# The eighth key group of the attention by seven products too, with another order of products and all four banks taken out by ScalarE

## The chip, the cores and the metric

The kernel runs on one core of a Trainium2 chip. Its engines work side by side, each through its own instruction queue in order: TensorE (PE in the profile; its weight loads are listed apart as PEld), VectorE (DVE), ScalarE (ACT), GpSimd (POOL) and SyncE (SP), which here only issues DMAs. SBUF is the working memory; PSUM holds what TensorE writes. The metric is the device time in microseconds of one execution; before the change it is 3199.19 us, the median of three runs (3198.45 to 3201.14).

## The reference

Two layers on an input x of 4 x 256 x 64 x 64, all fp32. Layer 0 is a self-attention over the N = 4096 positions of an image; layer 1 is a clustering block with an MLP and two pointwise convolutions, which the change hardly touches.

```python
xf = x.reshape(B, Cc, N)
q = jnp.einsum('oc,bcn->bno', wq, xf) + bq
k = jnp.einsum('oc,bcn->bon', wk, xf) + bk[None, :, None]
attn = jax.nn.softmax(jnp.einsum('bnd,bdm->bnm', q, k), axis=-1)
v = jnp.einsum('oc,bcn->bon', wv, xf) + bv[None, :, None]
out = jnp.einsum('bcn,bmn->bcm', v, attn).reshape(B, Cc, H, W)
return gamma[0] * out + x
```

## The kernel before

**Tiling.** An image (batch) is worked as 8 query blocks of 512 queries (`NB`); each block goes through 8 key groups of 512 keys (`RG` = 4 tiles of 128 keys). One block with one group is a unit: 64 units per image, numbered u, with block nb = u // 8 and group g = u % 8. The four images follow one another. While one image is in its clustering block and MLP, the values and first scores of the next are worked in between.

**A unit's life.** `half` (L452) computes half of a unit's scores, two matmuls (`products`, L420); ScalarE copies them to an SBUF slot (`kept`, L433), and VectorE folds them into a running maximum (`highest_of`, L444). The score PSUM pool has two buffers, and one of them is held for the whole attention by the tile `hold`, so there is one buffer left for scores: the next score matmuls wait for copy and maximum. Scores run up to 11 units ahead; `at` says at which point of which unit each half is due (two per unit, three in four early ones). When a block's maxima are complete, `fold`, `highest` and `rows` bring the maximum across the partitions by way of a DMA through DRAM, and `known` (L566, ScalarE) copies it to `hold[:, 0]`; for block 1, `spread` does it with TensorE instead.

**Weights of the softmax.** `exps(u)` subtracts the maximum (L583, VectorE, two instructions) and takes the exponentials (ScalarE). `factors(u)` makes what the products need: t31 (L616, VectorE, which also reads `hold[:, 1]`), the B12 sum, t4 and the row sums `one` and `both` (POOL, L595). t31 has two buffers, t4 one.

**Seven products.** For groups 0 to 6 the product of values and weights, split into 2 x 2 quarters, is done with seven quarter products instead of eight (a Strassen-Winograd scheme). `weigh(u, av, part)` issues them in four parts, (1, 5), (7, 2), (6, 4), (3), each product as two 128x256 matmuls, which the profile counts as four records (L679). They are summed in four PSUM banks over the groups of the block. Their key-side sums (`sums`, POOL) are made once per image. Group 7 is multiplied plainly: 128x512 matmuls (L657), into banks 2 and 3 only.

**Taking the banks out.** Banks 0 and 1 are complete after group 6. At the start of unit 7 `evict` (L699, ScalarE) scales both into an SBUF tile, `combine` (L709 to L712, four operations) adds the quarters up, on POOL in blocks 0 to 5 and on VectorE in blocks 6 and 7, and `gather` (POOL) ends the row sums. Banks 2 and 3 are added by `complete` (L724, VectorE), half at the end of unit 7, half in the next block's unit 0. `total`, `leave` and `sent` then divide by the row sums and send the block out to DRAM in units 1 to 5 of the next block. In block 7 the end differs: no scores are due, inputs are loaded back with an accumulating DMA that POOL issues (L772, L777), VectorE takes statistics, and the row sums are turned by two small TensorE products (L1003, L1017).

**Order.** The whole order is written by hand in `weighting` (L881): for each unit, which instruction is issued before which. In unit u stand, in turn: scores due at part 0, evictions and `gather` (unit 7), `exps(u + 1)`, maxima, part 0 of the products, scores due at part 1, part 1, scores due at part 2, `known` (unit 6), `factors(u + 1)`, maxima, part 2, `leave` and `sent`, part 3, `tail`. Waits between engines are set by the framework from what each instruction reads and writes.

Of the kernel before, what the change touches and what calls it, by code (L numbers as in the profile page):

```python
# [8 lines left out]
F32 = mybir.dt.float32  # L9
# [24 lines left out]

SEVEN = 7
QW = NB // 2
B21, B11, B12, B22 = range(4)
PAIR = slice(B11, B12 + 1), slice(B21, B22 + 1, 3)


PC = [
# [12 lines left out]
def attention_then_cluster_block(  # L54
# [250 lines left out]
    def attention(b, xs, ys):  # L305


        own = {}
        stats = small.tile([P, 2 * NBLK, 6], F32, tag="stats", name=f"st1_{b}")
        cells = small.tile([P, KC, NBLK, 4], F32, tag="cells", name=f"cells_{b}")  # L310
        qs, ks, slots, mxs, accs, tops, rdens, ts = {}, {}, {}, {}, {}, {}, {}, {}
# [265 lines left out]
        def exps(u, between=lambda: None):  # L577

            s = slots[u]
            mb = own["hold"][:, 0].rearrange("p (h n) -> p h n", h=2).unsqueeze(2)  # L580
            for j in range(2):
                sh = s[:, PAIR[j]]
                nc.vector.tensor_tensor(sh, sh, mb.to_broadcast([P, 2, 2, QW]), ALU.subtract)  # L583
                if j == 0:
                    between()
            if u % GRP < SEVEN:
                b12 = own["hold"][:, 1].rearrange("p (r n) -> p r n", r=2)
                nc.scalar.activation(b12, s[:, B12], AF.Exp)  # L588
                nc.scalar.activation(s[:, B11], s[:, B11], AF.Exp)  # L589
            else:  # L590
                nc.scalar.activation(s[:, PAIR[0]], s[:, PAIR[0]], AF.Exp)
            nc.scalar.activation(s[:, PAIR[1]], s[:, PAIR[1]], AF.Exp)  # L592
# [4 lines left out]
        def factors(u):  # L597

            nb, g = divmod(u, GRP)
            s = slots[u]
            if g == 0:
                accs[nb] = work.tile([P, 2, 2, QW], F32, tag="acc", bufs=1, name=f"acc_{b}_{nb}")
            one, both = accs[nb][:, 0], accs[nb][:, 1]
            if g >= SEVEN:
                if g == SEVEN:
                    plus(both, both, one, ALU.subtract)
                for acc, q in ((both, B11), (one, B12), (both, B21), (one, B22)):
                    eng = nc.vector if acc is one and nb == NBLK - 1 else nc.gpsimd  # L610
                    eng.tensor_tensor(acc, acc, s[:, q], ALU.add)  # L611
                return
            b12 = own["hold"][:, 1].rearrange("p (r n) -> p r n", r=2).unsqueeze(1)
            t31[u] = work.tile([P, 2, 2, QW], F32, tag="t13", name=f"t13_{b}_{u}")
            t4s[u] = work.tile([P, 2, QW], F32, tag="t4", bufs=1, name=f"t4_{b}_{u}")
            nc.vector.tensor_tensor(  # L616
                t31[u], s[:, B11 : B22 + 1 : 2], b12.to_broadcast([P, 2, 2, QW]), ALU.add
            )
# [29 lines left out]
        def weigh(u, av, part):  # L648

            g, s = u % GRP, slots[u]  # L650
            if g >= SEVEN:
                c = part // 2
                for t in (0, 1) if part % 2 == 0 else (2, 3):

                    apart = c == 1 and g == SEVEN and t == 0
                    for h in (slice(0, 1), slice(1, 2)) if apart else (slice(0, 2),):
                        nc.tensor.matmul(  # L657
                            av[2 + c].rearrange("p (h n) -> p h n", h=2)[:, h],
                            own["v"][:, RG * g + t, c * P : (c + 1) * P],
                            s[:, PAIR[t // 2], t % 2][:, h],  # L660
                            start=False,
                            stop=(g == GRP - 1 and t == RG - 1),
                        )
                return
            a11, a12, a21, a22 = left(g)
# [9 lines left out]
            }  # L675
            for i in ((1, 5), (7, 2), (6, 4), (3,))[part]:
                bank, half_, a, t = terms[i]
                for r in range(2):
                    nc.tensor.matmul(  # L679
                        av[bank][:, half_ * QW : (half_ + 1) * QW],  # L680
                        a[:, r],
                        t[:, r],
                        start=(g == 0 and r == 0 and i in (1, 7, 2, 4)),
                        stop=(g == SEVEN - 1 and r == 1 and i in (5, 6)),
                    )
# [8 lines left out]
        def evict(nb, av, i):  # L694


            if i == 0:
                ts[nb] = work.tile([P, 4, QW], F32, tag="t", bufs=1, name=f"t_{b}_{nb}")
            nc.scalar.activation(  # L699
                ts[nb][:, (slice(0, 4, 3), slice(1, 3))[i]],  # L700
                av[i].rearrange("p (h n) -> p h n", h=2),
                AF.Identity,
                scale=pvc("gamma"),
            )

        def combine(nb, eng):

            t = ts[nb]
            eng.tensor_tensor(t[:, 1], t[:, 1], t[:, 0], ALU.subtract)  # L709
            eng.tensor_tensor(t[:, 3], t[:, 1], t[:, 3], ALU.subtract)  # L710
            eng.tensor_tensor(t[:, 1], t[:, 1], t[:, 2], ALU.add)
            eng.tensor_tensor(t[:, 2], t[:, 2], t[:, 3], ALU.add)  # L712

        def complete(nb, av, c):

            t = ts[nb]
            for dst, src, op in (
                ((t[:, ::3], av[2].rearrange("p (h n) -> p h n", h=2), ALU.add),),
                (
                    (t[:, 1], av[3][:, :QW], ALU.subtract),  # L720
                    (t[:, 2], av[3][:, QW:], ALU.add),
                ),
            )[c]:
                nc.vector.scalar_tensor_tensor(dst, src, pvc("gamma"), dst, ALU.mult, op)  # L724

# [83 lines left out]
        def alone():  # L809
# [25 lines left out]
            fold(0)  # L835
            for g in range(4, SEVEN):
                for f in sums(g):
                    f()
# [8 lines left out]
            exps(0)  # L847
            factors(0)

        def maximum():  # L850
# [30 lines left out]
        def weighting(next_x, fill, early, begin):  # L881

            mb, av, den, peak = None, None, iter(()), iter(())

# [22 lines left out]
            for u in range(units):  # L907
# [5 lines left out]
                if g == 0:  # L913
                    done, av = av, [
                        pool.tile([P, NB], F32, tag=tag, name=f"av{c}_{b}_{nb}")
# [19 lines left out]

                if nb and g == 0:
                    complete(nb - 1, done, 1)
                elif nb and g == 1:
                    den = total(nb - 1)
# [54 lines left out]
                if g == GRP - 1 and more:  # L994
                    complete(nb, av, 0)
                tail(u)
# [36 lines left out]
        parts.ys, parts.alone, parts.weighting = ys, alone, weighting  # L1033
        parts.factors, parts.sums = factors, [lambda g=g, i=i: sums(g)[i]() for g in range(SEVEN) for i in range(4)]
        parts.score, parts.fold, parts.q_block, parts.k_unit = score, fold, q_block, k_unit
# [10 lines left out]
    def cluster(b, ys, stats, cells, rest, fill, gelu, nxt, maxima, turn):  # L1046
# [278 lines left out]
        fill(0 if nxt else 1)  # L1325
        stats2 = small.tile([P, 2 * NBLK, 6], F32, tag="stats", name=f"st2_{b}")
        pieces = {}
# [186 lines left out]
    def mlp(b, ys, stats2, fill, nxt, blocks, turned, maxima):  # L1514
# [314 lines left out]
        for nb in range(blocks):  # L1829
            end = nb == blocks - 1  # L1830
            for j in range(4):
# [12 lines left out]
                if nxt and nb:  # L1844
                    for _ in range(2 if j == 0 else 1):
                        if nxt.sums:
# [192 lines left out]
```

## Time and profile before

| what | value |
|---|---|
| median of three runs | 3199.19 us |
| the profiled execution | 3196.98 us |
| its span, first to last instruction | 3195.0 us |
| mean granted TensorE clock | 0.990 |
| POOL operation 128x512 (L595, into acc) | 352 of 1329 ns |
| POOL operation 128x256 (L709, L711, L712) | 24 each of 727 to 730 ns |
| VectorE t31 (L616) | 224 of 1217 ns |
| ScalarE eviction (L699) | 64 of 689 ns |
| plain products of group 7 (L657) | 448 of 592 ns, 128 of 378 ns |
| an average middle query block | 57.8 us |

A profile page lists for each engine its busy time and its share of the span. A timeline line gives the start in us, the duration in us, the engine, the line of the kernel, the operation, what it writes and reads, the shape and how many instructions are merged; in brackets stands how long the engine had been idle and what ended that. The granted clock is the share of full speed that TensorE was given. All fences marked as profile are copied from the profile and not shortened.

### The profile page before, as it was taken

The page shows a single profiled execution, that of the slowest core. Times are in us where ns is not written, and L with a number is a line of the kernel's source. Part 1 is how long each engine was busy: PE and PEld are TensorE (multiplying, and loading weights), DVE is VectorE, ACT ScalarE, POOL GpSimd, SP SyncE. Part 2 cuts the span into 40 slices and gives each one's busy share as a digit, 9 for nine tenths or more (in the row PEclk, how much of TensorE's full clock was granted, in tenths as well). Part 3 has the DMA queues.
Part 4 walks back from the last instruction along what each step waited for, and adds up shares of the span by engine and source line. Part 5 has one row for each costly group of instructions (what it writes and reads, how often), then busy time and mean ns, then how long its engine had stood idle before and what let it go on. Part 6 is the DMA issues. An engine that isn't in the chain of part 4 may idle for free.

```text
span 3195.0 us, 40473 instructions
## 1 busy us (share of the span) xinstructions
PE 3085.5 (97%) x13890; PEld 2445.7 (77%) x13890; DVE 2537.0 (79%) x3649; ACT 1734.8 (54%) x2719; POOL 2260.6 (71%) x2127
## 2 busy tenths in 40 slices
PE   7999999999999999999999999999999999998999
PEld 5777887788677787768867788786876787875786
DVE  3888888677788888867778888877778888887675
ACT  4556654545556665445555666544556566654444
POOL 3888886378488888547848888855766888883663
PEclk8999999999999999999999999999999999999999
DMA  5122126100112123510011222431111112150000
GB/s 164 40 63 63 60 61 182 63 21 30 47 50 63 53 60 94 155 50 28 23 56 44 66 60 63 111 123 50 30 44 43 54 60 64 56 149 2 14 21 27
DMA packets 105868, 200.33 MB, mean 63 GB/s; under 512 B 14416, under 2 KB 30400, under 8 KB 104128
## 3 DMA queue, kind: packets, MB, share of 16 engines
q1 hardware_dynamic: 101856, 181.94, 17.9%
q0 software_dynamic: 2976, 14.70, 2.5%
q8 instruction: 110, 1.80, 0.2%
q10 hardware_dynamic: 832, 1.11, 0.1%
q14 instruction: 94, 0.77, 0.1%
HBM read 149.37 MB, written 48.34 MB: 62 GB/s over the span
## 4 chain that ended last, share of the span: by engine, by line
PE 42%; POOL 24%; DVE 19%; issue 8%; ACT 6%; DMA 1%; POOLq 0%; SPq 0%; ACTq 0%; DVEq 0%
PE mo L1651 10%; POOL acc L595 9%; PE av L679 6%; PE hq L1734 5%; DVE top L444 5%; DVE s L583 4%; POOL t L595 4%; POOL s L595 4%; DVE t L616 3%; PE hp L1734 3%; PE hr L1734 3%; PE fv L1225 3%; PE sc L420 3%; POOL acc L611 2%; PE vp L375 2%
## 5 line engine op out<-in xcount | busy, mean ns | idle before, releaser
L433 ACT COPY s<-sc 128x1024 f32<-128x1024 f32 x512 | 514.8, 1011 | 506.3 <-PE sc L420 500.1
L583 DVE TENSOR_TENSOR s<-s,hold 128x1024 f32<-128x1024 f32 x512 | 598.7, 1209 | 28.9 <-ACT hold L566 15.0
L595 POOL TENSOR_TENSOR s<-t,s 128x512 f32<-128x512 f32 x224 | 303.5, 1355 | 356.1 <-DVE t L616 287.6
L679 PE MATMUL av<-t,v 128*128 128x256 f32 x1792 | 464.8, 382 | 12.8 <-DVE t L616 11.7
L679 PE MATMUL av<-s,v 128*128 128x256 f32 x1792 | 460.8, 379 | 2.2 <-ACT s L589 2.2
L595 POOL TENSOR_TENSOR acc<-acc,t 128x512 f32<-128x512 f32 x352 | 461.2, 1329 | 0.0
L679 PE MATMUL av<-s,sum 128*128 128x256 f32 x1792 | 459.5, 379 | 0.0
L420 PE MATMUL sc<-q,k 128*128 128x512 f32 x1024 | 405.6, 480 | 36.8 <-DMA k<-k 10.5
L444 DVE TENSOR_TENSOR top<-sc,top 128x1024 f32<-128x1024 f32 x326 | 397.8, 1220 | 29.7 <-ACT s L433 24.8
L1689 ACT ACTIVATE hs<-hs,pv_s 128x256 f32<-128x256 f32 x496 | 232.3, 502 | 343.5 <-DVE hs L1725 343.5
L616 DVE TENSOR_TENSOR t<-s,hold 128x1024 f32<-128x1024 f32 x224 | 272.7, 1217 | 159.3 <-ACT s L592 71.0
L679 PEld LDWEIGHTS av<-t,v 128*128 128x128 f32 x1792 | 338.4, 190 | 70.1 <-DVE t L616 21.4
L1651 PE MATMUL mo<-hs,w 128*128 128x256 f32 x1512 | 385.3, 381 | 0.0
L679 PEld LDWEIGHTS av<-s,v 128*128 128x128 f32 x1792 | 340.3, 190 | 57.8 <-ACT s L589 2.6
L679 PEld LDWEIGHTS av<-s,sum 128*128 128x128 f32 x1792 | 339.4, 189 | 54.5 <-issue 1.9
L1651 PEld LDWEIGHTS mo<-hs,w 128*128 128x128 f32 x1512 | 283.0, 190 | 47.2 <-ACT hs L1689 6.4
L595 POOL TENSOR_TENSOR t<-s 128x512 f32<-128x512 f32 x224 | 295.7, 1320 | 17.6
L420 PEld LDWEIGHTS sc<-q,k 128*128 128x128 f32 x1024 | 176.6, 190 | 144.0 <-DVE top L444 70.2
L592 ACT ACTIVATE s<-s 128x1024 f32<-128x1024 f32 x256 | 267.5, 1045 | 1.2
L1725 DVE TENSOR_TENSOR hs<-hq,hs 128x256 f32<-128x256 f32 x496 | 198.8, 421 | 79.2 <-PE hq L1734 69.3
L588 ACT ACTIVATE hold<-s 128x512 f32<-128x512 f32 x224 | 135.1, 603 | 221.5 <-DVE s L583 221.4
L679 PE MATMUL av<-t,sum 128*128 128x256 f32 x896 | 231.7, 381 | 0.0
(299 smaller groups left out, 5349.1 us busy)
## 6 DMA issues: line engine op xcount, KB each, us to landing
k<-k SPq DMA_DIRECT2D x256, 256.0 KB, 2.7
x<-in_x SPq DMA_DIRECT2D x62, 512.0 KB, 6.6
out<-xn SPq DMA_DIRECT2D x62, 256.0 KB, 2.1
att<-t SPq DMA_DIRECT2D x56, 256.0 KB, 3.9
x<-att POOLq DMA_DIRECT2D x12, 1024.0 KB, 8.7
q<-q SPq DMA_DIRECT2D x32, 256.0 KB, 4.1
w<-in_w SPq DMA_DIRECT2D x8, 1024.0 KB, 10.3
rden<-row_rd SPq DMA_DIRECT2D x28, 256.0 KB, 3.7
```

The lines of the kernel that those rows point to most:

```text
L420: nc.tensor.matmul(sc[:, r, :], k_s[:, (2 * h + r) * P : (2 * h + r + 1) * P], qs[u // GRP], start=True, stop=True,)
L433: nc.scalar.copy(slots[u][:, PAIR[h]].rearrange("p h r n -> p r h n"), tiles(sc))
L444: nc.vector.tensor_tensor(top, src, top if saved[nb] is None else saved[nb], ALU.max)
L583: nc.vector.tensor_tensor(sh, sh, mb.to_broadcast([P, 2, 2, QW]), ALU.subtract)
L592: nc.scalar.activation(s[:, PAIR[1]], s[:, PAIR[1]], AF.Exp)
L595: nc.gpsimd.tensor_tensor(out, x, y, op)
L616: nc.vector.tensor_tensor(t31[u], s[:, B11 : B22 + 1 : 2], b12.to_broadcast([P, 2, 2, QW]), ALU.add)
L679: nc.tensor.matmul(av[bank][:, half_ * QW : (half_ + 1) * QW], a[:, r], t[:, r], start=(g == 0 and r == 0 and i in (1, 7, 2, 4)), stop=(g ...
L1651: return nc.tensor.matmul(bank[:, half * HB : (half + 1) * HB], a[:, j], t, start=start, stop=stop)
L1689: nc.scalar.activation(src, src, AF.Gelu_apprx_tanh, bias=pvc("b1", P, j + 4 * (i > 1)))
L1725: nc.vector.tensor_tensor(dst, ps, term, ALU.add)
L1734: nc.tensor.matmul(out, w, x, start=True, stop=True)
```

## The change

Group 7 is now treated like the others; the special case and its constant go.

- `exps`: group 7 too takes B12's exponential into `hold[:, 1]`: two instructions of 512 in place of one of 1024.
- `factors`: for group 7 t31 on VectorE and four sums on POOL in place of four row-sum additions on POOL (two of them on VectorE in block 7). The last subtraction `both - one` moves from before these to behind them.
- `weigh`: seven products in group 7; the parts become (1, 5), (2, 3), (7, 6), (4), and in an image's last unit (7, 6), (1, 5), (2, 3), (4). Banks 0, 2, 1, 3 are then complete after parts 0, 1, 2, 3 of unit 7.
- In blocks 0 to 6 four evictions on ScalarE, one behind each part of unit 7; the fourth takes half a bank. The quarters are combined by six POOL operations, two at the end of each of units 0, 1 and 2 of the next block. VectorE's completions and its combine of block 6 go.
- In block 7 banks 1 and 0 are evicted behind parts 0 and 1, VectorE combines, and completes with two operations in place of three.
- Four more key-side sums per image: at the start for image 0, in the MLP for the others, where now two sums instead of one are issued at j = 1.
- `stats` and `cells` get one buffer instead of two; a tile `t5` is new, and `w2` serves a further use.

```diff
+ORDER = (1, 5), (2, 3), (7, 6), (4,)
+LAST = (7, 6), (1, 5), (2, 3), (4,)
...
-            if u % GRP < SEVEN:
-                b12 = own["hold"][:, 1].rearrange("p (r n) -> p r n", r=2)
-                nc.scalar.activation(b12, s[:, B12], AF.Exp)
-                nc.scalar.activation(s[:, B11], s[:, B11], AF.Exp)
-            else:
-                nc.scalar.activation(s[:, PAIR[0]], s[:, PAIR[0]], AF.Exp)
+            b12 = own["hold"][:, 1].rearrange("p (r n) -> p r n", r=2)
+            nc.scalar.activation(b12, s[:, B12], AF.Exp)
+            nc.scalar.activation(s[:, B11], s[:, B11], AF.Exp)
             nc.scalar.activation(s[:, PAIR[1]], s[:, PAIR[1]], AF.Exp)
...
-            if g >= SEVEN:
-                if g == SEVEN:
-                    plus(both, both, one, ALU.subtract)
-                for acc, q in ((both, B11), (one, B12), (both, B21), (one, B22)):
-                    eng = nc.vector if acc is one and nb == NBLK - 1 else nc.gpsimd
-                    eng.tensor_tensor(acc, acc, s[:, q], ALU.add)
-                return
...
+            if g == GRP - 1:
+                plus(both, both, one, ALU.subtract)
...
-            for i in ((1, 5), (7, 2), (6, 4), (3,))[part]:
+            for i in (ORDER if u < units - 1 else LAST)[part]:
...
+        def combined(nb):
+
+            t = ts[nb]
+            yield from combine(nb, nc.gpsimd)
+            yield nc.gpsimd.tensor_tensor(t[:, ::3], t[:, ::3], ts.pop((nb, 2)), ALU.add)
+            yield nc.gpsimd.tensor_tensor(t[:, 1], ts.pop((nb, 3))[:, 0], t[:, 1], ALU.subtract)
...
-                if g == SEVEN:
-                    evict(nb, av, 0)
-                    evict(nb, av, 1)
-                    if nb < NBLK - 2:
-                        combine(nb, nc.gpsimd)
+                if g == GRP - 1:
                     gather(nb)
                 if g + 1 < GRP or more:
                     exps(u + 1)
-                if g == SEVEN and nb >= NBLK - 2:
-                    combine(nb, nc.vector)
...
                 weigh(u, av, 0)
+                if g == GRP - 1:
+                    evict(nb, av, 0 if more else 1)
...
                 weigh(u, av, 1)
...
-                if g == GRP - 1 and not more:
-                    complete(nb, av, 0)
+                if g == GRP - 1:
+                    evict(nb, av, 2 if more else 0)
+                    if not more:
+                        for _ in combine(nb, nc.vector):
+                            pass
...
                 weigh(u, av, 2)
+                if g == GRP - 1:
+                    if more:
+                        evict(nb, av, 1)
+                    else:
+                        complete(nb, av, 0)
...
                 if g == GRP - 1 and more:
-                    complete(nb, av, 0)
+                    evict(nb, av, 3)
+                    quarters = combined(nb)
+                elif nb and g < 3:
+                    for _ in range(2):
+                        next(quarters)
                 tail(u)
```

More of the change, by code (lines that the diff above doesn't have):

```diff
@@ L31 @@
 LEAD, SLOTS = 11, 10
-SEVEN = 7
 QW = NB // 2
@@ L308, in attention @@
         own = {}
-        stats = small.tile([P, 2 * NBLK, 6], F32, tag="stats", name=f"st1_{b}")
-        cells = small.tile([P, KC, NBLK, 4], F32, tag="cells", name=f"cells_{b}")
+        stats = small.tile([P, 2 * NBLK, 6], F32, tag="stats", bufs=1, name=f"st1_{b}")
+        cells = small.tile([P, KC, NBLK, 4], F32, tag="cells", bufs=1, name=f"cells_{b}")
         qs, ks, slots, mxs, accs, tops, rdens, ts = {}, {}, {}, {}, {}, {}, {}, {}
@@ L650, in weigh @@
             g, s = u % GRP, slots[u]
[L651 to L664, printed above, removed]
             a11, a12, a21, a22 = left(g)
@@ L683, in weigh @@
                         start=(g == 0 and r == 0 and i in (1, 7, 2, 4)),
-                        stop=(g == SEVEN - 1 and r == 1 and i in (5, 6)),
+                        stop=(g == GRP - 1 and r == 1 and i in (5, 3, 6, 4)),
                     )
@@ L694, in evict @@
         def evict(nb, av, i):
-            if i == 0:
+            if nb not in ts:
                 ts[nb] = work.tile([P, 4, QW], F32, tag="t", bufs=1, name=f"t_{b}_{nb}")
+            if i == 2:
+                ts[nb, 2] = work.tile([P, 2, QW], F32, tag="w2", bufs=1, name=f"t2_{b}_{nb}")
+            if i == 3:
+                ts[nb, 3] = work.tile([P, 1, QW], F32, tag="t5", bufs=1, name=f"t5_{b}_{nb}")
             nc.scalar.activation(
-                ts[nb][:, (slice(0, 4, 3), slice(1, 3))[i]],
-                av[i].rearrange("p (h n) -> p h n", h=2),
+                ts[nb, i] if i > 1 else ts[nb][:, (slice(0, 4, 3), slice(1, 3))[i]],
+                av[i][:, : QW if i == 3 else NB].rearrange("p (h n) -> p h n", n=QW),
                 AF.Identity,
@@ L708, in combine @@
             t = ts[nb]
[L709 to L712, printed above, removed]
+            yield eng.tensor_tensor(t[:, 1], t[:, 1], t[:, 0], ALU.subtract)
+            yield eng.tensor_tensor(t[:, 3], t[:, 1], t[:, 3], ALU.subtract)
+            yield eng.tensor_tensor(t[:, 1], t[:, 1], t[:, 2], ALU.add)
+            yield eng.tensor_tensor(t[:, 2], t[:, 2], t[:, 3], ALU.add)
+        def combined(nb):
[3 more added lines that the diff above has]
+            yield nc.gpsimd.tensor_tensor(t[:, 1], ts.pop((nb, 3))[:, 0], t[:, 1], ALU.subtract)
         def complete(nb, av, c):
             t = ts[nb]
[L717 to L724, printed above, removed]
+            dst, src, op = (
+                (t[:, ::3], av[2].rearrange("p (h n) -> p h n", h=2), ALU.add),
+                (t[:, 1], av[3][:, :QW], ALU.subtract),
+            )[c]
+            nc.vector.scalar_tensor_tensor(dst, src, pvc("gamma"), dst, ALU.mult, op)
         def total(nb):
@@ L835, in alone @@
             fold(0)
-            for g in range(4, SEVEN):
+            for g in range(4, GRP - 1):
                 for f in sums(g):
@@ L848, in alone @@
             factors(0)
+            for f in sums(GRP - 1):
+                f()
         def maximum():
@@ L881, in weighting @@
         def weighting(next_x, fill, early, begin):
-            mb, av, den, peak = None, None, iter(()), iter(())
+            mb, av, den, peak, quarters = None, None, iter(()), iter(()), iter(())
             views = {units - 7 + i: i for i in range(6)}
@@ L913, in weighting @@
                 if g == 0:
-                    done, av = av, [
+                    av = [
                         pool.tile([P, NB], F32, tag=tag, name=f"av{c}_{b}_{nb}")
@@ L934, in weighting @@
                     caught(1)
-                if nb and g == 0:
-                    complete(nb - 1, done, 1)
-                elif nb and g == 1:
+                if nb and g == 1:
                     den = total(nb - 1)
@@ L1033, in attention @@
         parts.ys, parts.alone, parts.weighting = ys, alone, weighting
-        parts.factors, parts.sums = factors, [lambda g=g, i=i: sums(g)[i]() for g in range(SEVEN) for i in range(4)]
+        parts.factors, parts.sums = factors, [lambda g=g, i=i: sums(g)[i]() for g in range(GRP) for i in range(4)]
         parts.score, parts.fold, parts.q_block, parts.k_unit = score, fold, q_block, k_unit
@@ L1325, in cluster @@
         fill(0 if nxt else 1)
-        stats2 = small.tile([P, 2 * NBLK, 6], F32, tag="stats", name=f"st2_{b}")
+        stats2 = small.tile([P, 2 * NBLK, 6], F32, tag="stats", bufs=1, name=f"st2_{b}")
         pieces = {}
@@ L1844, in mlp @@
                 if nxt and nb:
-                    for _ in range(2 if j == 0 else 1):
+                    for _ in range(2 if j < 2 else 1):
                         if nxt.sums:
```

## The prediction

> **What bounds the kernel.** I read the page's first part, then the timeline of single query blocks engine by engine, then the chain of waits inside one block.
>
> ```profile
> PE 3085.5 (97%) x13890; PEld 2445.7 (77%) x13890; DVE 2537.0 (79%) x3649; ACT 1734.8 (54%) x2719; POOL 2260.6 (71%) x2127
> ```
>
> 97% looks like a TensorE-bound kernel, but the records overlap: a 128x256 matmul "takes" 0.38 us while in the timeline four of them start every 0.86 us (331.73, 332.59, 333.45), 0.215 each. By starts, an attention unit (one key group for one query block) costs TensorE 28 x 0.215 = 6.04 us of products and 0.86 for its four score matmuls: 6.9. Its real period is in the timeline of VectorE and ScalarE, units 3 to 4 of batch 0's fourth block:
>
> ```profile
> 338.03 2.34 DVE L583 TENSOR_TENSOR s<-s,hold 128x1024 f32<-128x1024 f32 x2
> 340.29 1.22 DVE L444 TENSOR_TENSOR top<-sc,top 128x1024 f32<-128x1024 f32 x1
> 340.47 0.60 ACT L588 ACTIVATE hold<-s 128x512 f32<-128x512 f32 x1 [0.46 <-DVE s L583]
> 341.00 0.61 ACT L589 ACTIVATE s<-s 128x512 f32<-128x512 f32 x1
> 341.52 1.04 ACT L592 ACTIVATE s<-s 128x1024 f32<-128x1024 f32 x1
> 342.65 1.22 DVE L616 TENSOR_TENSOR t<-s,hold 128x1024 f32<-128x1024 f32 x1 [1.15 <-POOL acc L595]
> 343.89 1.23 DVE L444 TENSOR_TENSOR top<-sc,top 128x1024 f32<-128x1024 f32 x1
> ```
>
> The next subtraction starts at 345.03. A closed ring: subtract 2.34, exponentials 2.1, t sum 1.22, maximum 1.22, hand-overs 0.1: 7.0 us. (342.65 is put down to POOL, which ended at 341.99; the exponentials ended at 342.56.) So VectorE and ScalarE set 7.0, TensorE follows with 6.9, POOL needs four operations, 5.1. Three limits lie close together.
>
> **The removed work.** The eighth group's 18 matmuls (L657) run from 1265.69 to 1272.56, 6.87 us; seven products take 6.04. Saved: 0.83 us x 32 blocks = 26.6 us, if TensorE decided. The page's mean durations say the opposite: 14 x 592 + 4 x 378 ns = 9.8 us before against 28 x 380 = 10.6, which would be 27 us slower. [...] The starts in this trace agree, so I take minus 26.6 as what TensorE has to give. Whether it gets out depends on the ring, unit by unit.
>
> **Units 6 and 7 of blocks 1 to 5.** The timeline of VectorE and ScalarE before:
>
> ```profile
> 359.39 2.30 DVE L583 TENSOR_TENSOR s<-s,hold 128x1024 f32<-128x1024 f32 x2
> 361.62 1.21 DVE L444 TENSOR_TENSOR top<-sc,s 128x1024 f32<-128x1024 f32 x1
> 362.86 2.07 DVE L444 TENSOR_TENSOR top<-s,top 128x1024 f32<-128x1024 f32 x1
> 364.74 0.60 ACT L566 COPY hold<-mr 128x512 f32<-128x512 f32 x1
> 365.04 1.23 DVE L444 TENSOR_TENSOR top<-sc,top 128x1024 f32<-128x1024 f32 x1
> 366.18 2.34 DVE L583 TENSOR_TENSOR s<-s,hold 128x1024 f32<-128x1024 f32 x2
> 368.36 1.27 ACT L699 ACTIVATE t<-av,pv_s 128x512 f32<-128x512 f32 x2
> 371.71 1.22 DVE L616 TENSOR_TENSOR t<-s,hold 128x1024 f32<-128x1024 f32 x1 [1.98 <-ACT s L592]
> 374.27 0.75 DVE L724 SCALAR_TENSOR_TENSOR t<-av,pv_s,t 128x512 f32<-128x512 f32 x1 [0.21 <-POOL t L712]
> ```
>
> The next subtraction is at 374.94. Unit 6 is the one unit whose VectorE list is full (6.79 us) and it has no t sum, since unit 7 needs none. Unit 7 takes 8.76, because the two evictions (1.27) stand before the exponentials and a completion (0.75) follows.
> - Unit 7 after: no eviction ahead of the exponentials, no completion on VectorE. The ring is the ordinary 7.0. Gain 1.76. The evictions now follow the exponentials and the products they read, so ScalarE does them in the slack: two by 5.8 us after the unit's subtraction; behind them waits the second score copy (until 6.7), and behind it TensorE's next scores, which need the maximum at 7.07 anyway. Cost nothing; half a us later it would cost its excess.
> - Unit 6 after: VectorE gains the t sum, 1.22, with no gap to take it. And there is a new wait. The hold tile has two banks; ScalarE's copy L566 writes the first, the t sum reads the second. Are they kept apart? Row L588 above: it writes bank two and waits 0.46 us for the second subtraction, which only reads bank one. And at 729.83 a ScalarE copy of the first bank of an MLP tile starts only when the product in the other bank ends (729.17 + 0.59). So I take it that a PSUM tile is waited for whole, and the t sum comes behind L566, which comes behind the score copy: 5.95 to 6.05 us after the subtraction. Then 1.22 + 1.22 + hand-overs: 8.43 us instead of 6.79. Loss 1.64. If the banks are kept apart, the t sum starts at 5.54 and the unit takes 8.0.
> - Net per block: 1.76 - 1.64 = 0.1 gain (0.55 with banks apart). TensorE's saved 0.83 becomes idle time in unit 6 (some 1.9 us).
>
> **Block 0.** There the maximum comes over TensorE and VectorE idles 2.83 us in unit 6, so the t sum is hidden. Unit 7: 8.57 before; after 7.9, since a held maximum (1.76) fills the exponentials' shadow. Gain 0.6, less 0.1 in the next unit.
>
> **Block 6 into 7, and block 7.** Timeline of batch 1:
>
> ```profile
> 1266.30 2.35 DVE L583 TENSOR_TENSOR s<-s,hold 128x1024 f32<-128x1024 f32 x2 [3.68 <-ACT hold L566]
> 1275.73 1.13 PE L679 MATMUL av<-t,v 128*128 128x256 f32 x4 [2.14 <-DVE t L616]
> 1275.75 1.28 POOL L595 TENSOR_TENSOR s<-t,s 128x512 f32<-128x512 f32 x1 [1.50 <-DVE t L616]
> 1325.06 1.65 POOL L595 TENSOR_TENSOR rden<-acc 128x256 f32<-128x256 f32 x2
> ```
>
> Before, the combine sat on VectorE between subtraction and t sum (1268.64 to 1274.5) and TensorE lost 2.14 us. It goes to POOL; that stall goes. What is late next: eviction 0 stands on ScalarE behind the exponentials and the shift (2.17), and the t sum of unit 7 behind L566, now about 1267.45 because the new exponential order starts after both subtractions. TensorE then waits about 2.2 us for that t sum, and 2.1 us for eviction 0 (1276.0) before block 7's first product. It starts block 7 about 1 us later than before.
>
> Then POOL. Added in block 7: the combine, 4 x 0.73 + 1.33 + 0.75 = 5.0 us in units 0 to 2, and for the eighth group five operations (6.4) in place of one and two (1.59 + 3.45). POOL's idle time in block 7 before was 1.50 + 1.77 + 0.57 + 1.25 + 1.27 + 0.26 = 6.6; block 7 has no scores, units last 6.36, and POOL also issues three back-transfers (0.9 each) and one of 1.08, and does the 2.36 scaling. Walking its queue from 1268.8 with 1.27 per operation, it is busy without a gap from unit 57 on: its B12 sum for the last unit ends near 1323.0, where TensorE, through with the first product of the last list (7, 6), waits some 2 us. The last product ends near 1328.2 (1326.2 before), the row sums (1325.06 + 1.65 before) near 1330.4, the next value projection at about 1331.3 instead of 1328.36. Loss 2.9 us a batch. With banks apart the same walk starts 2.7 earlier and ends with 1.1 lost. The back-transfers are issued up to 4 us later; who needs them first, the pooling of unit 57, reads at about 1284, and the t sum behind it has 3 us of slack.
>
> **The rest.** Four more key-side sums per batch (0.8 us each): in the MLP they go to POOL, which waits 73 us there for TensorE; nothing, at worst 1 us a batch. At the start they fall into a 3.25 us POOL gap. Product order: 4 is now last, so POOL's next t4 waits for the unit's end (about 7.15 us after the subtraction) and would start at 7.28: nothing, by 0.1 us. Single buffers for the statistics: their lives follow one another; nothing.
>
> **The sum.** Per batch: -0.5 - 5 x 0.1 + 2.9 = +1.9; four batches +7.6 us. The profiled execution took 3196.98 (span 3195.0), which becomes 3204.6; that execution lies 2.2 under the median of 3199.19, so 3206.8, say **3207**.
>
> **Rivals.**
> - *TensorE decides* (10%): the ring's slack swallows the t sum, 0.83 gained in every block: 3199.2 - 26.6 = 3172.6. For it: page 97%. Against: unit 6, where TensorE waits for VectorE (the scores at 366.62 came 0.6 late).
> - *Banks kept apart* (15%), on the faster side: the t sum of unit 6 doesn't wait for L566. Per batch -0.5 - 5 x 0.55 + 1.1 = -2.15; 3190.6. It decides from the point at which the t sum starts before 5.95 us of its unit. Against: L588's wait.
> - *POOL's overrun is absorbed* (15%): block 7 loses 1 us instead of 2.9 because back-transfers issue beside other work: about 3199.
> - *The clock drops* (12%): batch 0's gap of 2.20 us was followed by groups of four at 1.97 and 1.91 instead of 1.03, clock 0.83 in that stretch; 2.14 in batch 1 was not. [...] by batch 0's row some 1.75 us each. In half of 24 gaps: +21, 3228. [...] three of the four 2.1 us gaps left no trace.
> - Forecast: 48%, own range 3200 to 3216.
>
> No change means within 0.2%, 6.4 us, which is what a measurement here can tell. Faster 10 + 15 = 25%; same: the absorbed case and a fifth of the forecast, 26%; slower 49%. Range 3186 to 3223: it leaves out the first rival and most of the clock case.
>
> **What would show it.** Unit 6 of blocks 1 to 5 near 8.4 us between subtractions with the t sum right after L566, unit 7 near 7.0; TensorE idle about 1.9 us before unit 7's scores; in block 7 POOL without gaps and the row sums some 3 us later. Wrong: unit 6 below 7.5, or block 7's last product no later than now.

## The result, and the profile after

The changed kernel takes **3241.0 us** (median of four runs, 3239.64 to 3243.07), beside 3199.4 us for the kernel before on the same chip: a ratio of 1.0128, interval 1.0116 to 1.014. It is 42 us slower, where 8 us were forecast; the time lies above the forecast's range. The profiled execution has a span of 3237.8 us, 42.8 more than before.

The first part of its page, busy time of each engine:

```profile
PE 3068.9 (95%) x14210; PEld 2504.8 (77%) x14210; DVE 2502.2 (77%) x3569; ACT 1772.2 (55%) x2807; POOL 2323.0 (72%) x2223
```

PE and VectorE lost busy time, ScalarE gained 37 us, POOL 62; none of the four is busy all the time. So busy times don't explain the 42.8 us, and they are looked for unit by unit. As in the prediction, a unit runs from one subtraction (L586, once L583) to the next. The table sums over the four images how each place differs between the two profiled executions, beside what the prediction's steps make of it. (Its own sum rounds these steps to +7.6.) Each entry is rounded by itself.

| place | forecast, us | measured, us |
|---|---|---|
| unit 7 of blocks 1 to 5 (20 units) | -35.2 | -19.9 |
| unit 6 of blocks 1 to 5 (20 units) | +32.8 | +35.4 |
| block 0 | -2.0 | -0.7 |
| blocks 6 and 7, to the next value projection or the end | +11.6 | +8.9 |
| block 1, other units | 0 | +5.5 |
| blocks 2 to 6, other units | 0 | +3.4 |
| clustering and MLP of images 0 to 2 | 0 | +7.0 |
| before the first subtraction | 0 | +3.1 |
| sum | +7.2 | +42.8 |

A middle block goes from 57.77 to 58.45 us: unit 6 from 6.79 to 8.30, unit 7 from 8.76 to 7.76 instead of 7.0. The timeline of VectorE, ScalarE and TensorE for units 6 and 7 of a middle block of image 1 shows both:

```profile
1106.50 2.30 DVE L586 TENSOR_TENSOR s<-s,hold 128x1024 f32<-128x1024 f32 x2
...
1111.83 0.59 ACT L569 COPY hold<-mr 128x512 f32<-128x512 f32 x1
1112.52 1.22 DVE L609 TENSOR_TENSOR t<-s,hold 128x1024 f32<-128x1024 f32 x1 [0.49 <-ACT hold L569]
1114.80 2.34 DVE L586 TENSOR_TENSOR s<-s,hold 128x1024 f32<-128x1024 f32 x2
...
1119.24 1.25 ACT L686 ACTIVATE t<-av,pv_s 128x512 f32<-128x512 f32 x2
1119.42 1.22 DVE L609 TENSOR_TENSOR t<-s,hold 128x1024 f32<-128x1024 f32 x1 [1.15 <-POOL acc L595]
1120.38 1.01 ACT L436 COPY s<-sc 128x1024 f32<-128x1024 f32 x1
1121.42 1.22 DVE L447 TENSOR_TENSOR top<-sc,top 128x1024 f32<-128x1024 f32 x1 [0.77 <-ACT s L436]
1122.56 2.34 DVE L586 TENSOR_TENSOR s<-s,hold 128x1024 f32<-128x1024 f32 x2
```

Unit 6 (from 1106.50): the t sum starts right behind ScalarE's copy into the hold tile, as forecast. Unit 7 (from 1114.80): VectorE is through with its t sum at 1120.64 and wants the second maximum. This starts at 1121.42, when ScalarE's copy of the same scores ends (1121.39); the copy had stood in ScalarE's queue behind the two evictions (L686). In 84 maxima of image 1 that read scores in PSUM, none starts before the end of the last copy begun before it; the smallest distance is 0.03 us. (At the start of image 0, before the hold tile takes one of the two score buffers, four maxima do run beside a copy: that of the other buffer.)

Two other places, first unit 1 of block 1, POOL and VectorE:

```profile
952.62 0.72 POOL L696 TENSOR_TENSOR t<-t 128x256 f32<-128x256 f32 x1
953.42 0.73 POOL L697 TENSOR_TENSOR t<-t 128x256 f32<-128x256 f32 x1
954.09 0.42 POOL L529 MEMSET few<- 128x384 f32 x1
954.55 0.69 DVE L535 TENSOR_REDUCE few<-few 128x16 f32<-128x512 f32 x1 [2.41 <-POOL few L529]
```

Once an image POOL zeroes the small reduction tile, when `total` first asks for it. The first two combining operations now stand ahead of it, and VectorE waits 2.41 us; in the trace of before the same reduction waited 0.91. The longer wait recurs in all four images.

Second, the view of waits for VectorE, in all of the changed kernel (engine, line, what it waited for, us in total, times, longest), and then two rows of before:

```profile
DVE top L447 <- ACT s L436: 38.6, 39, 2.2
DVE t L609 <- ACT hold L569: 35.0, 24, 4.8
DVE xn L1724 <- POOL xn L1616: 31.1, 15, 2.1
```

```profile
DVE top L444 <- ACT s L433: 26.7, 31, 2.6
DVE xn L1725 <- POOL xn L1617: 15.6, 12, 1.3
```

Maxima waited for copies before the change too, at other places. In the units 7 of blocks 1 to 5 such waits came to 3.4 us before, 6 times; now every one of the 20 units has one, 17.6 us in all. The third row is the MLP: VectorE waits twice as long as before for POOL's normalisation, in whose queue the second key-side sum of step 1 now stands.

### The profile page after: what moved, and what is told of

It is laid out like the page before. It is cut to its first block, busy times and chain, and to the rows that moved or that the text cites. A ratio compares the mean times of both kernels' runs of the same rounds, so it can differ in the third digit from the quotient of the medians.

```text
span 3237.8 us, 41259 instructions
## 1 busy us (share of the span) xinstructions
PE 3068.9 (95%) x14210; PEld 2504.8 (77%) x14210; DVE 2502.2 (77%) x3569; ACT 1772.2 (55%) x2807; POOL 2323.0 (72%) x2223
## 4 chain that ended last, share of the span: by engine, by line
PE 54%; DVE 15%; POOL 13%; ACT 10%; issue 6%; DMA 2%; ACTq 0%; SPq 0%; POOLq 0%; DVEq 0%
PE av L661 16%; PE mo L1650 10%; PE hq L1733 5%; POOL acc L595 5%; DVE top L447 4%; DVE s L586 4%; PE sc L423 4%; PE hp L1733 3%; PE hr L1733 3%; POOL t L595 3%; PE fv L1224 3%; PE vp L378 3%; ACT s L436 2%; ACT s L592 2%; POOL s L595 2%
## 5 line engine op out<-in xcount | busy, mean ns | idle before, releaser
L586 DVE TENSOR_TENSOR s<-s,hold 128x1024 f32<-128x1024 f32 x512 | 598.6, 1209 | 8.3 <-PE hold L576 8.3
L595 POOL TENSOR_TENSOR s<-t,s 128x512 f32<-128x512 f32 x256 | 345.4, 1349 | 315.5 <-DVE t L609 243.4
L661 PE MATMUL av<-t,v 128*128 128x256 f32 x2048 | 532.0, 382 | 14.0 <-DVE t L609 12.6
L595 POOL TENSOR_TENSOR acc<-acc,t 128x512 f32<-128x512 f32 x416 | 541.9, 1323 | 0.0
L661 PE MATMUL av<-s,v 128*128 128x256 f32 x2048 | 530.5, 382 | 7.1 <-ACT t L686 5.0
L661 PE MATMUL av<-s,sum 128*128 128x256 f32 x2048 | 527.1, 380 | 9.8 <-POOL s L595 9.8
L609 DVE TENSOR_TENSOR t<-s,hold 128x1024 f32<-128x1024 f32 x256 | 311.7, 1218 | 217.3 <-ACT s L592 64.7
L661 PEld LDWEIGHTS av<-t,v 128*128 128x128 f32 x2048 | 389.8, 191 | 77.4 <-DVE t L609 16.5
L661 PEld LDWEIGHTS av<-s,v 128*128 128x128 f32 x2048 | 390.2, 191 | 71.1 <-ACT t L686 6.5
L661 PEld LDWEIGHTS av<-s,sum 128*128 128x128 f32 x2048 | 389.0, 190 | 66.2 <-POOL s L595 13.4
L595 POOL TENSOR_TENSOR t<-s 128x512 f32<-128x512 f32 x256 | 332.7, 1300 | 47.0 <-PE av L661 33.7
## 6 DMA issues: line engine op xcount, KB each, us to landing
w<-in_w SPq DMA_DIRECT2D x8, 1024.0 KB, 11.6
```

The costliest lines, as they stand in the source:

```text
L595: nc.gpsimd.tensor_tensor(out, x, y, op)
L609: nc.vector.tensor_tensor(t31[u], s[:, B11 : B22 + 1 : 2], b12.to_broadcast([P, 2, 2, QW]), ALU.add)
L661: nc.tensor.matmul(av[bank][:, half_ * QW : (half_ + 1) * QW], a[:, r], t[:, r], start=(g == 0 and r == 0 and i in (1, 7, 2, 4)), stop=(g ...
```

## The experiments

Each edit is made to the changed kernel. The runs were spread over several chips; on these the kernel before took 3197.7 to 3200.6 us, and single times of one kernel lie up to 9 us apart. So a few us in the last column are not told by the time alone.

The "closing stretch" runs from the start of unit 6 of block 6 to the next value projection: 68.0 to 68.4 us before and 70.8 after, alike in images 0 to 2. The time from an image's last subtraction alone is less sure a measure: in the same three images of the changed kernel it is 15.5, 17.0 and 17.6 us.

| run | median, us | against 3241.0 |
|---|---|---|
| evictions behind the score copy | 3223.35 | -17.7 |
| hold copy behind the t sum | 3217.26 | -23.7 |
| zeroing early | 3236.62 | -4.4 |
| MLP's extra sum in step 2 | 3230.61 | -10.4 |
| block 6 combined on VectorE | 3262.87 | +21.9 |
| maximum written ahead of the copy | 3246.88 | +5.9 |
| the first four together | 3183.85 | -57.2 |
| the four, a row sum on VectorE | 3185.27 | -55.7 |
| the four, the held maximum split | 3180.71 | -60.3 |

**Evictions behind the score copy.**

```diff
                 weigh(u, av, 0)
-                if g == GRP - 1:
-                    evict(nb, av, 0 if more else 1)
+                if g == GRP - 1:
+                    if not more:
+                        evict(nb, av, 1)
...
                 maxima = due(u, 2)
+                if g == GRP - 1 and more:
+                    evict(nb, av, 0)
+                    evict(nb, av, 2)
```

> The changed kernel with evictions 0 and 2 of unit 7 put behind the second score copy in ScalarE's queue instead of ahead of it (blocks 0 to 6). Theory A, the evictions are the cost: the second maximum of unit 7 waits for ScalarE's copy of the same score tile, and that copy stands behind 1.25 us of evictions. Then the 0.77 us wait in front of the maximum goes, unit 7 falls from 7.76 to 7.0 us in 28 blocks, 28 x 0.76 = 21 us: about 3220. Rival B, the maximum waits for late scores of TensorE and the copy only ends beside it: unit 7 stays at 7.7, 3241. Rival C, the evictions now end in unit 0 of the next block and hold up its first products: unit 7 at 7.0 but unit 0 up by as much, 3235 to 3241.

Unit 7 falls to 7.01 us in blocks 1 to 5 and unit 0 stays at 7.0: theory A, 17.7 us of the 21. It was counted for 28 units, but unit 7 of blocks 0 and 6 had no such wait and stays as it was; 20 times 0.75 us are 15. The timeline of unit 7:

```profile
1111.40 1.22 DVE L609 TENSOR_TENSOR t<-s,hold 128x1024 f32<-128x1024 f32 x1 [1.14 <-POOL acc L595]
1111.60 1.01 ACT L436 COPY s<-sc 128x1024 f32<-128x1024 f32 x1 [0.28 <-PE sc L423]
1112.51 2.22 ACT L686 ACTIVATE t<-av,pv_s 128x512 f32<-128x512 f32 x4
1112.64 1.23 DVE L447 TENSOR_TENSOR top<-sc,top 128x1024 f32<-128x1024 f32 x1
```

The copy now runs beside the t sum and the maximum follows without a wait; the next subtraction starts at 1113.79, 7.01 us after the last. All four evictions are done 0.94 us into the next unit, before its exponentials. So the evictions do fit into ScalarE's slack; only their place was dear.

**Maximum written ahead of the copy.** Is it the copy, or ScalarE's queue in general? Here only the order in which the two readers of the score tile are written is turned.

```diff
             sc = products(u, h)
+            if copy_last:
...
+                return lambda: (highest_of(nb, tiles(sc)), kept(u, h, sc))
             kept(u, h, sc)
...
-            fs = [half(p, h, kept_only)]
+            fs = [half(p, h, kept_only, part == 2 and u % GRP == GRP - 1)]
```

> The changed kernel with one thing turned round in unit 7: the second maximum is written ahead of ScalarE's copy of the same score tile. The order of instructions within each engine is the same as before the turn, the evictions still stand ahead of the copy; only which of the two readers of the tile waits for the other can change. Theory A, two readers of one PSUM tile on two engines go one after the other in the order in which they are written: the maximum no longer waits, starts right behind the t sum, and unit 7 falls from 7.76 to about 7.0; the copy then ends about 1 us later than the maximum did, so TensorE's next scores, which need the tile free, come up to 1 us late in unit 0 of the next block, where VectorE has 1.15 us of room: 3220 to 3230. Rival B, the maximum waits for ScalarE's evictions or for TensorE, not for the copy: unit 7 stays at 7.76, 3241. Rival C, the late scores cost unit 0 as much as unit 7 gains: 3241.

Unit 7 falls to 6.9 us, as theory A has it, and unit 0 grows from 7.0 to 8.05, as rival C has it, by more than was gained: 5.9 us slower. The timeline of VectorE, ScalarE and TensorE at the seam:

```profile
1120.91 1.25 ACT L689 ACTIVATE t<-av,pv_s 128x512 f32<-128x512 f32 x2
1122.24 1.22 DVE L447 TENSOR_TENSOR top<-sc,top 128x1024 f32<-128x1024 f32 x1
1123.49 1.01 ACT L436 COPY s<-sc 128x1024 f32<-128x1024 f32 x1 [1.33 <-DVE top L447]
1124.55 0.73 PE L423 MATMUL sc<-q,k 128*128 128x512 f32 x2 [0.70 <-ACT s L436]
```

The maximum goes first and the copy waits 1.33 us for it: here two engines that only read one PSUM tile go one after the other, in the order in which the kernel writes them, with 0.77 us of wait one way round and 1.33 the other.

**Hold copy behind the t sum.**

```diff
-                if more and nb and g == GRP - 2:
-                    known(mb)
                 if g + 1 < GRP or more:
                     factors(u + 1)
+                if more and nb and g == GRP - 2:
+                    known(mb)
```

> The changed kernel with the copy of the new maximum into the first bank of the hold tile emitted behind the t sum of unit 7, which reads the second bank, instead of ahead of it. Theory A, a PSUM tile is waited for whole: the t sum loses its wait of 0.49 us for the copy, unit 6 of blocks 1 to 5 falls from 8.31 to 8.0 us (20 x 0.3 = 6 us), and in block 6, where the copy comes late (wait up to 4.8 us), the t sum of its last unit comes some 2.7 us earlier, of which up to 2 us reach the end of block 7: 4 x 2 = 8. Together 3227 to 3235. Rival B, the t sum waits for the exponentials and VectorE's own queue and the copy only ends beside it: unit 6 stays at 8.3, 3241. Rival C, the copy now stands behind the t sum and the next subtraction comes later by what the t sum saves: 3241 to 3245.

Theory A in kind, and the largest single gain, 23.7 us against the 14 at most that were expected. The timeline of unit 6 (its subtraction at 1097.65):

```profile
1103.11 1.21 DVE L609 TENSOR_TENSOR t<-s,hold 128x1024 f32<-128x1024 f32 x1
1104.35 0.59 ACT L569 COPY hold<-mr 128x512 f32<-128x512 f32 x1 [1.26 <-DVE t L609]
```

Now the copy into bank one waits 1.26 us for the t sum, which only reads bank two: here the tile is waited for whole, either way round (0.49 us the other way, in the changed kernel). Units 6 of blocks 1 to 5 lose 17.3 us in sum instead of 6, for two reasons. The expectation counted instructions by their durations of 1.22 us, but in a row they start 1.13 us apart (1.14 in the changed kernel), so unit 6 takes 7.72 us and not 8.0. And the copy depends on a DMA: in image 3 of the changed kernel it came late (0.72 us of wait for the DMA at 2680.27), and unit 6 grew there to 8.7 to 9.9 us in blocks 1 to 4. With the copy behind the t sum such a delay is mostly covered: in image 3 blocks 3 to 5 take 57.9 us instead of 58.8 to 60.3; in block 1 it reappears in unit 7 (10.0 us). The end of block 7 gained too: unit 6 of block 6 falls from 8.27 to 7.08, and the closing stretch from 70.8 to 68.4, 70.0 and 68.4 us in images 0 to 2. With image 3, taken to the end of the program, that is 6.6 us of the 8 expected.

**Zeroing early.**

```diff
+                if u == GRP - 2:
+                    spare()
                 if g == GRP - 1:
                     gather(nb)
```

> The changed kernel with the zeroing of the small reduction tile (POOL, once a batch) emitted in unit 6 of block 0 instead of in unit 1 of block 1, where it stands behind the first two combining operations of POOL. Theory A, the reduction of unit 1 in block 1 waits 2.41 us for that zeroing: the wait goes, block 1 falls from 65.5 to about 63.1 us or less (62.8 before the change), 4 x 2.4 = 10 us at most, 4 x 1.65 = 6.6 if the 0.9 us that it waited before the change is hidden otherwise: 3231 to 3235. Rival B, block 1 is longer for another reason (held maxima, the denominator's DMA): block 1 stays at 65.5, 3241.

(`spare` makes the tile and zeroes it when it is first called.) Block 1 falls from 65.5 to 63.3 us in images 1 and 2 and unit 1 from 10.04 to 7.79: theory A in the trace, with no wait of the reduction left. The median falls by 4.4 us, less than what these runs can tell by the time alone; the block's times carry the verdict.

**The MLP's extra sum in step 2.**

```diff
-                    for _ in range(2 if j < 2 else 1):
+                    for _ in range(2 if j % 2 == 0 else 1):
```

> The changed kernel with the second key-side sum of each MLP block put into step 2 (where POOL waited 1.5 us for ScalarE) instead of step 1 (where POOL's queue runs without a gap into the normalisation). Theory A, the extra sum of step 1 is what makes the MLP longer by some 3 us in batches 0 and 1 and 1 us in batch 2: from the first value projection behind the attention to the next batch's first subtraction 314 us again instead of 317 (290 instead of 291): 3 + 3 + 1 = 7 us, about 3234. Rival B, the MLP is longer for another reason (its inputs, the output's DMA): 317 stays, 3241. Rival C, step 2 is as tight as step 1: 317, 3241.

From the value projection to the next image's first subtraction the profiled execution takes 315.9, 313.7 and 289.5 us instead of 317.1, 316.8 and 290.8, 5.6 us in sum, and VectorE's wait for POOL is back at what it was before:

```profile
DVE xn L1724 <- POOL xn L1616: 15.7, 12, 1.3
```

Theory A: six profiled executions without this edit take 316.6 us or more in images 0 and 1, the four with it at most 315.9. The median fell by 10.4 us, more than this place gives; the rest is not explained.

**Block 6 combined on VectorE.** The six operations of units 0 to 2 of block 7 move from POOL to VectorE.

```diff
+            eng = nc.gpsimd if nb < NBLK - 2 else nc.vector
-            yield from combine(nb, nc.gpsimd)
+            yield from combine(nb, eng)
```

(The two operations behind it take the same engine.)

> The changed kernel with the six combining operations of block 6 (they fall into units 0 to 2 of block 7) on VectorE instead of POOL. Theory A, POOL's overrun in block 7 sets the end of the attention: POOL is relieved of 6 operations, some 5 us, its last sum comes earlier, and from the last subtraction to the next value projection it takes 14 to 14.5 us instead of 17.0: 4 x 2.7 = 11 us, about 3230. Rival B, the operations on VectorE delay its subtractions and t sums by their own 3 to 4 us and block 7 grows from 45.4 to 48 us: no gain, 3238 to 3245. Rival C, the tail is set by the last product and the row sums whatever POOL did before: tail stays near 17.0, 3241.

Rival B, and far worse than it said: block 7 grows from 45.4 to 52.7 us. VectorE in the second unit:

```profile
1307.54 1.10 DVE L696 TENSOR_TENSOR t<-t 128x256 f32<-128x256 f32 x1
1308.67 2.08 DVE L697 TENSOR_TENSOR t<-t 128x256 f32<-128x256 f32 x1
```

Two 128x256 operations take 3.2 us, where the first of the same operations at the end of block 7 takes 0.42 (1347.65 in the changed kernel), and the next subtraction, at 1310.68, stands behind them. The closing stretch grows from 70.8 us to between 76.2 and 76.6. From the last subtraction it is 15.3 us instead of 17.0 in image 1, but that subtraction itself comes later here, so the run does not show what relieving POOL is worth alone.

**The four together.** The four edits that helped.

> The changed kernel with four moves together: evictions 0 and 2 behind the score copy, the hold copy behind the t sum, the zeroing early, the MLP's extra sums in step 2. Theory A, the four costs lie one behind the other and add up: 3241 - 18 - 24 - 4 - 7 = 3188, units 6 and 7 of blocks 1 to 5 at 7.7 and 7.0 us. Rival B, removing one exposes another (TensorE's 6.9 us a unit, POOL's four operations): the gains overlap and the time stays at 3195 to 3205, about that of the kernel before.

3183.85 us: 57.2 less than the changed kernel, against a sum of single gains of 56.2, so they hardly overlap, as far as runs on different chips can tell. Against the kernel before the ratio is 0.9956 (0.9944 to 0.9969): this version beats both. A middle block takes 57.1 us, unit 6 7.75 and unit 7 7.01.

**A row sum on VectorE.** In the last unit of an image the sum into `one` moves from POOL to VectorE.

> As the run with the four moves, and the one sum of the last unit of block 7 that feeds only the row sums is made by VectorE, which is through with its own work there. Theory A, POOL's queue sets the row sums and these the next value projection: the row sums end 1.3 us earlier and the value projection comes up to 1.3 us earlier in batches 0 to 2; some 4 us less than the run with the four moves. Rival B, the projection waits for the last products and the completion, not for the row sums: nothing.

The closing stretch takes 67.7 to 68.0 us in images 0 to 2, in the run with the four moves 70.1, 68.4 and 68.4; the row sums end 2.9, 0.9 and 0.8 us earlier in it. That is theory A in kind; the time is 3185.27 (3181.12 to 3189.69), which can't be told from the 3183.85 without it.

**The held maximum split.** The one maximum from SBUF that stands in unit 6 (2.07 us) is made in two halves, in units 6 and 7.

```diff
...
+                    for r in range(2):
+                        held.append(lambda r=r: higher(nb, own_copy, r))
...
-                if nb < 2 or g == 6:
+                if nb < 2 or g >= 6:
                     caught(1)
```

> As the run with the four moves, and in blocks 2 to 5 the held maximum of 2.07 us is made in two halves, one in unit 6 and one in unit 7, each in the 1.15 us in which VectorE waits for the exponentials. Theory A, VectorE's list is what sets unit 6 at 7.7: unit 6 falls to 7.0 and unit 7 stays at 7.0, 16 x 0.7 = 11 us less than the run with the four moves, about 3177. Rival B, TensorE or POOL is next: unit 6 stays above 7.4 or unit 7 grows; less than 5 us.

Unit 6 falls from 7.75 to 7.21 us with unit 7 at 7.0, some 0.5 of the 0.7 expected, so VectorE's list does set unit 6. The time falls by 3.1 us to 3180.71 (ratio to before 0.9944, 0.9931 to 0.9958), less than the 11 expected and within what two runs of one kernel differ by: not shown in the time. In the profiled execution units 6 gain 8.9 us, but units 7 lose 2.8 and the closing stretch is 1.7 us longer in images 1 and 2; why is not shown.

## Why the prediction was wrong

**The step that failed** is the one on the evictions of unit 7: "behind them waits the second score copy (until 6.7), and behind it TensorE's next scores, which need the maximum at 7.07 anyway. Cost nothing". The timing was right: the copy ended 6.59 us after the subtraction. The user was wrong. The step named TensorE as the one that waits behind the copy; the maximum itself does, because it reads the tile that the copy reads, and it is wanted at 5.84. It cost 0.75 us in each of the units 7 of blocks 1 to 5 and made 15.3 us of the 35.6 us by which the measured change exceeds the forecast. That it is the copy was shown by turning the two readers round, with the evictions left in their place. The prediction had the observation in hand: for the hold tile it took a PSUM tile to be waited for whole, but it asked this only of a writer and a reader and never of two readers.

**Unit 6**: right in mechanism and size, 8.30 against 8.43 us, with the t sum behind L569. It is the largest loss of the change, 44.4 us with block 6, and it came with a weakness that the sum lacked: the t sum now waits for a DMA too, which made units 6 longer than 8.30 in images 0 and 3, some 5 us of the 35.4. The rival *banks kept apart* is refuted from both sides (0.49 us and 1.26 us of wait). Moving the copy, an edit that the prediction did not think of, takes 23.7 us off. Two separate tiles in place of the one hold tile were not tried.

**TensorE decides**: refuted. Its saved 0.83 us a block turned into idle time: before unit 7's scores it waited 1.46 us for the maximum (1.9 forecast).

**Blocks 6 and 7**: +8.9 us against +11.6: 2.7, 2.7 and 2.4 in images 0 to 2, near the 2.9 forecast, and 1.2 in image 3, behind which no projection comes. The row sums ended 3.1 to 3.2 us later in images 0 to 2 (some 3 forecast), so the rival *POOL's overrun is absorbed*, with 1 us a batch, did not come true there. TensorE waited 1.99 us for the t sum of unit 7 (2.2 forecast), 1.66 for eviction 0 (2.1), and 1.78 for POOL's B12 sum in the last unit (2):

```profile
1344.03 1.13 PE L661 MATMUL av<-s,sum 128*128 128x256 f32 x4 [1.78 <-POOL s L595]
...
1352.11 1.99 PE L378 MATMUL vp<-wv_s,x 128*128 128x256 f32 x8 [0.72 <-DVE t L715]
```

**What was costed at nothing.** Three terms of zero were not zero. The combining operations on POOL in block 1: the walk through POOL's queue was made for block 7 alone, and in block 1 the zeroing stands behind them (6.7 us in unit 1; the rest of the block is some 1.1 us shorter, 5.5 in all). The MLP's sums: "POOL, which waits 73 us there for TensorE; nothing, at worst 1 us a batch"; it waits there in sum, but in step 1 of an MLP block it has no gap, and 7.0 us were lost. The start: "they fall into a 3.25 us POOL gap"; they did, but beside them ran VectorE's small preparations, and the unit grew by 1.9 us (last section), which lies within block 0's -0.7. The 3.1 us before the first subtraction are largely the first load, for which TensorE waited 8.8 us before the change and 10.6 after; in the nine profiled executions of its variants it was 9.6 to 11.3, so no cause in the change is shown. The 3.4 us in blocks 2 to 6 are unit 0, 6.84 to 7.0 us: its first scores used to start 0.81 us ahead of its subtraction and now start 0.13 behind it. Whether that is the cause was not tried apart.

**The clock** rival happened in part; its weight, a drop in half of 24 gaps at 12 per cent, was the author's estimate. Groups of four products that took over 1.3 us instead of 1.03 cost 9.5 us in excess after and 4.7 before. It is a small share, but in image 3 late hold copies opened gaps of 2.36 and 1.88 us behind which the granted clock fell to 0.50 (last section).

The prediction's chances for "same" and "slower" come to 25 and 50 per cent by its own list, not 26 and 49; nothing rests on it.

## What to carry to other kernels

When an engine's queue gets new work, ask of each instruction behind it not only who takes its result but who shares its tile: here a second reader of the same PSUM tile waited as well (0.77 or 1.33 us), and so did a reader of its other bank (0.49 us) or, the other way round, the writer (1.26 us); the order in which the kernel writes them decided who. An average of idle time ("POOL waits 73 us in this stage") hides nothing by itself; walk the queue at every place where the new instructions land. Where a moved instruction costs, try it a few lines further on before giving the change up: four moves, none of which removes work, turned 1.3% slower into 0.4% faster.

## What the runs showed of the hardware

**Clock.** In this trace idle time of TensorE alone does not say whether the granted clock drops. Two gaps in image 3 of the changed kernel:

```profile
2563.70 0.74 PE L423 MATMUL sc<-q,k 128*128 128x512 f32 x2 [3.13 <-DVE top L447]
2564.28 1.02 PE L661 MATMUL av<-s,v 128*128 128x256 f32 x4
...
2742.20 0.73 PE L423 MATMUL sc<-q,k 128*128 128x512 f32 x2 [1.88 <-DVE top L447]
...
2743.82 1.91 PE L661 MATMUL av<-t,v 128*128 128x256 f32 x4
```

After 3.13 us the first four products take 1.02, and the granted clock is 1.00 from 2560 to 2571; after 1.88 us the second four take 1.91, and the granted clock is 0.50 from 2743.45 for 3.4 us. In this trace drops followed gaps of 1.88, 2.00, 2.36 and 4.10 us, and none followed others of 1.88 and 2.00, or those of 2.29, 2.41 and 3.13. What decides between two gaps of 1.88 us, no run shows.

**VectorE beside POOL.** In the first unit of image 0 VectorE does small operations on 128x2 elements. Before, with POOL idle beside them, such an operation takes 0.16 us:

```profile
80.87 0.16 DVE L241 TENSOR_TENSOR dw_e<-dw_d,pc_s 128x2 f32<-128x2 f32 x1
```

In the changed kernel POOL makes its four added sums there, and the same operation takes 0.65:

```profile
83.88 0.72 POOL L595 TENSOR_TENSOR sum<-v 128x256 f32<-128x256 f32 x1
83.97 0.65 DVE L244 TENSOR_TENSOR dw_e<-dw_d,pc_s 128x2 f32<-128x2 f32 x1
```

Each of the four sums has one such operation beside it (0.58 to 0.69 us); together they are 1.9 us longer, by which the unit grew. Each ends 0.02 us behind the sum beside it. The combine on VectorE was slow likewise: 1.10 and 2.08 us in block 7 of the experiment, and in the trace of before, at the end of block 6 of image 1, four operations of 0.76, 1.38, 1.38 and 2.27 us from 1268.64 on, with POOL busy beside them for most of that time. What makes them longer, no run here shows.
